# Scoring and summing units of 16 neighbour slots or more in two parts, in both graph-attention layers

## The chip, the cores and the metric

The program runs on one core of a Trainium2 chip. The metric is the device time of one execution in microseconds. Engines are named as in the profile: PE (TensorE, matmuls; PEld its weight loads), DVE (VectorE), ACT (ScalarE), POOL (GpSimd, which here issues the gathers), SP (SyncE, which issues plain DMAs).

## The reference

Two graph-attention layers over 2048 nodes, 8 batches of 256 features, with one adjacency matrix that is sparse (a few to some 36 neighbours a node). Cut to what matters:

```python
def _L0_gnn_ref(inp, adj, W1, W2, W3):
    e = jnp.einsum('bnd,bmd->bnm', inp @ W1, inp @ W2)
    e = jax.nn.leaky_relu(e, 0.2)
    e = jnp.where(adj[None, :, :] > 0, e, NEG_INF)
    attention = jax.nn.softmax(e, axis=-1)
    return jax.nn.relu(jnp.einsum('bnm,bmd->bnd', attention, inp @ W3))

def _L1_gnn_ref(h, adj, W, a):
    q = (h @ W).reshape(B, N, H, D)
    e = e_src[:, :, None, :] + e_dst[:, None, :, :]
    e = jnp.where(e >= 0, e, 0.2 * e)
    e = jnp.where(mask, e, NEG_INF)
    attn = jax.nn.softmax(e, axis=2)
    h_prime = jnp.einsum('bijh,bjhd->bihd', attn, q)
    return jax.nn.elu(h_prime.reshape(B, N, H * D))

x = _layernorm(x + _L0_gnn_ref(x, adj, W1, W2, W3))
x = _layernorm(x + _L1_gnn_ref(x, adj, W, a))
```

## The kernel before

**Units and slots.** The nodes are sorted by their number of neighbours and cut into 16 tiles of 128 nodes. `SLOTS` says how many neighbours the fullest node of each tile may have: 36, 24, 22, 21, 20, 19, 19, 18, 17, 17, 16, 15, 15, 14, 13, 12. A *slot* of a tile is one neighbour of each of its 128 nodes; nodes with fewer neighbours have masked slots, for which `neg` (one value per node and slot) holds a huge negative number and otherwise 0. The batches are taken in two halves of four. A *unit* (`Unit`, L438) is one tile of one half in one layer: 64 units, 2 x 2 x 298 slots in all. Layer 0 takes the tiles from the smallest to the largest, first for one half of the batches and then for the other; layer 1 takes a mixed order, with the 36-slot tile in the middle.

**Gathers and the ring.** A unit's neighbour rows come from DRAM by indirect DMAs that POOL issues, one per slot (128 rows of 4 KB), two slots to a chunk (`chunk_job`, L466; `gather`, L196). A chunk lies in one of 16 ring buffers (`RING`), and is given back once its slots are summed (`credits`). So at most 32 slots are in flight, scored and waiting, or being summed. `pump` (L477) issues gathers as long as there are credits.

**Scoring.** In layer 0 (`logits0`, L552) DVE takes, per slot and batch, the product of the gathered row with the node's own transformed row `u.g` and sums it into one score (L568: a custom operation and a read of its accumulator). When a part's slots are all scored, a chain of small operations makes the softmax: leaky ReLU (L581), the mask added (L582), maximum (L586), subtraction (L587), Exp on ACT (L588), sum (L591), reciprocal and division (L593, L594). In layer 1 (`logits1`, L765) the score is an addition of precomputed terms (L780), 16 values per slot, and the same chain follows at L788 to L810; the probabilities are also copied to PSUM (`pw`, L800).

**Summing.** In layer 0 (`sums0`, L654) ACT writes, per slot, four diagonal matrices from the probabilities (L665, four buffers of one slot each), and PE multiplies the gathered rows with them into PSUM accumulators, 16 matmuls a slot (L645). In layer 1 (`sums1`, L818) the gathered rows are weighted in place, four chunks of five by DVE (L846) and each fifth by ACT (L842), and PE adds them up, 8 matmuls a slot. The accumulators are two PSUM banks a part, from a pool of four.

**Parts.** A unit is split into two parts where it has more than 24 slots: the 36-slot tile alone, 18 + 18. Each part then has its own maximum, unnormalised probabilities and accumulators, and `shares` (L600) computes both parts' factors at the end of the unit, has PE move them to the order of the accumulators' rows (L620), and both accumulators are scaled and added (L683 to L691; L866 to L879). An unsplit unit's accumulators are copied out by ACT in layer 0 (L680) and read directly in layer 1 (L884, L892).

**What follows a unit.** `after0` (L695) transposes the sums, projects them with W3, adds the residual (L705), normalises, computes the layer-1 rows and scatters them (L204). `after1` (L863) does ELU, residual and layer norm and scatters the output. `before0` (L530) prepares the own rows of a unit.

**Order.** `tick` (L961) is called after each summed slot; it issues gathers, advances scoring by up to two steps while fewer than `limit` slots are scored ahead of the sums, and advances the work before and after units. A chunk is scored no earlier than 3 (layer 0) or 5 (layer 1) ticks after its gather. POOL's order is that of the program text; on the other engines a list scheduler fills gaps from this order when the program is built. The call at L998 gives the limit: rest of the unit + the next unit + 5.

Of the kernel before, what the change touches and what calls it, by code (L numbers as in the profile page):

```python
# [38 lines left out]
RING = 16  # L39
LEAD = 5  # L40
# [89 lines left out]
def fast_path(  # L130
# [307 lines left out]
    class Unit:  # L438
        def __init__(self, layer, h, t):
# [3 lines left out]

            n = self.K if self.K <= RING * CHUNK * 3 // 4 else -(-self.K // 2)
            self.parts = [(k, min(n, self.K - k)) for k in range(0, self.K, n)]
# [106 lines left out]
    def logits0(u):  # L552
# [3 lines left out]
        for i, (k0, K) in enumerate(u.parts):  # L556
            n, o = f"{u.name}_{i}", offs[u.t] + k0
            e = ep.tile([P, HB, K], F32, tag="e", name=f"e_{n}")
            for k in range(K):
# [6 lines left out]
                for b in range(HB):  # L566
# [6 lines left out]
                        scalar=0.0,  # L573
                        op0=ALU.mult,
                        op1=ALU.add,
                        accum_out=e[:, b, k : k + 1],
                    )
                yield 1
            p = e
            wide = [P, HB, K]  # L580
            nc.vector.scalar_tensor_tensor(p, e, ALPHA, e, ALU.mult, ALU.max)  # L581
            nc.vector.tensor_tensor(  # L582
                p, p, neg[:, o : o + K].unsqueeze(1).to_broadcast(wide), ALU.add
            )
            m = sp.tile([P, HG], F32, tag="m1", name=f"m_{n}")[:, :HB]
            nc.vector.tensor_reduce(m, p, AX.X, ALU.max)  # L586
            nc.vector.tensor_tensor(p, p, m.unsqueeze(2).to_broadcast(wide), ALU.subtract)  # L587
            nc.scalar.activation(p, p, AF.Exp)  # L588
            yield 0
            sm = sp.tile([P, HG], F32, tag="s1", name=f"s_{n}")[:, :HB]  # L590
            nc.vector.tensor_reduce(sm, p, AX.X, ALU.add)  # L591
            if len(u.parts) == 1:
                nc.vector.reciprocal(sm, sm)  # L593
                nc.vector.tensor_tensor(p, p, sm.unsqueeze(2).to_broadcast(wide), ALU.mult)  # L594
# [5 lines left out]
    def shares(u, G):  # L600


        f = sp.tile([P, 2, HG], F32, tag="f", name=f"f_{u.name}", bufs=1)[:, :, :G]
        top = sp.tile([P, HG], F32, tag="top", name=f"top_{u.name}", bufs=1)[:, :G]
        nc.vector.tensor_tensor(top, u.m[0], u.m[1], ALU.max)
        for i in range(2):
            nc.vector.tensor_tensor(f[:, i, :], u.m[i], top, ALU.subtract)
        nc.scalar.activation(f, f, AF.Exp)
        for i in range(2):
            nc.vector.tensor_tensor(u.s[i], u.s[i], f[:, i, :], ALU.mult)  # L610
        nc.vector.tensor_tensor(top, u.s[0], u.s[1], ALU.add)
        nc.vector.reciprocal(top, top)
        nc.vector.tensor_tensor(f, f, top.unsqueeze(1).to_broadcast([P, 2, G]), ALU.mult)
        fs = sp.tile([P, 2, 2, HG // 2], F32, tag="fs", name=f"fs_{u.name}", bufs=1)
        fs = fs[:, :, :, : G // 2]
        for r in range(2):
            rr = slice(64 * r, 64 * r + 64)
            pf = ps_tile(f"ps_f_{u.name}_{r}")[:, :G].rearrange("p (i g) -> p i g", i=2)
            for c in range(2):
# [3 lines left out]
                    rhs=f[rr, :, ts(c, G // 2)],  # L623
# [4 lines left out]
            nc.vector.tensor_copy(fs[:, :, r, :], pf)  # L628
# [25 lines left out]
    def sums0(u):  # L654
        accs = []
        for i, (k0, K) in enumerate(u.parts):
# [3 lines left out]
            for k in range(K):  # L660
# [10 lines left out]
                if s == n - 1:  # L671
                    credits[0] += 1
                yield 1
            accs.append(acc)

        def evict():
            u.hs = hsp.tile([P, HC], F32, tag="hs", name=f"hs_{u.name}")
            if len(accs) == 1:
                for r in range(2):
                    nc.scalar.copy(u.hs[:, ts(r, HW)], accs[0][r])  # L680
                return
            fs = shares(u, HB)
            for r in range(2):  # L683
                for j in range(2):
                    v = u.hs[:, ts(2 * r + j, C)]
                    nc.scalar.activation(
                        v, accs[0][r][:, ts(j, C)], AF.Copy, scale=fs[:, 0, r, j : j + 1]
                    )
                    nc.vector.scalar_tensor_tensor(
# [614 lines left out]
```

## Time and profile before

| | us |
|---|---|
| median of 14 runs (2641.13 to 2659.82) | 2648.78 |
| the profiled execution | 2650.9 |
| its span, first to last instruction | 2649.1 |
| layer 0 sums, first half of the batches | 170 to 885 |
| layer 0 sums, second half | 885 to 1548 |
| layer 1 sums | 1548 to 2626 |

| engine | busy us | share of the span |
|---|---|---|
| PE | 2090.0 | 79% |
| DVE | 2013.1 | 76% |
| ACT | 1445.0 | 55% |
| POOL | 1520.0 | 57% |

| group | count | busy us | mean ns of one |
|---|---|---|---|
| L568 DVE product and sum, layer 0 | 2384 | 858.5 | 419 |
| L645 PE sums, layer 0 | 9536 | 749.6 | 409 |
| L645 PE sums, layer 1 | 4768 | 847.1 | 672 |
| L846 DVE weighting, layer 1 | 260 | 573.9 | 2228 |
| L665 ACT diagonals, layer 0 | 2384 | 623.4 | 337 |
| L196 POOL gathers, layer 0 / layer 1 | 596 / 596 | 626.3 / 603.9 | 1051 / 1013 |

The stages are read off the sums' matmuls (L645): the first of layer 0 starts at 169.7 us, the first of the second half at 892.1, the first of layer 1 at 1552.3, the last ends at 2625.5. In a row, instructions of one engine overlap a little, so that the mean of one is longer than the time from one start to the next; busy time counts no moment twice. The wait lines give the engine, its line and tile, what ended the wait, the total in us, how often, and the longest. POOL's busy time holds only the issuing of the DMAs, not their transfers.

### The profile page before, as it was taken

What the parts mean: (1) busy time and instruction counts of PE and PEld (TensorE: products, weight loads), DVE (VectorE), ACT (ScalarE), POOL (GpSimd) and SP (SyncE); (2) the same over time, 40 slices, a digit from 0 to 9 for tenths busy, and PEclk for the clock granted to TensorE, in tenths of its full rate; (3) what the DMA queues carried; (4) which work ended last, traced back from release to release, by engine and by line L of the source; (5) the groups of instructions that cost most, each with busy time, mean ns of one, the idle gap of its engine ahead of it and who ended that gap; (6) DMA issues with size and microseconds to landing.
All of it is one profiled execution on the core that took longest, in us unless ns stands there. A gap on an engine that the chain in (4) does not pass through costs nothing.

```text
span 2649.1 us, 52177 instructions
## 1 busy us (share of the span) xinstructions
PE 2090.0 (79%) x16675; PEld 1105.6 (42%) x16675; DVE 2013.1 (76%) x7073; ACT 1445.0 (55%) x4849; POOL 1520.0 (57%) x1486
## 2 busy tenths in 40 slices
PE   0148889888889888889988888877877778887885
PEld 0135555555555555555555533322323223332223
DVE  7779687777878676677878667778877787887886
ACT  6135565655666566766666765442455545542544
POOL 3454455545556444555555647676676666665664
PEclk9578899889999899999999988888889898887888
DMA  9777788878786677888988678877898899868883
GB/s 378 277 266 250 270 287 279 268 273 277 261 294 221 215 241 261 280 296 271 303 293 266 233 251 309 311 289 261 291 322 310 293 327 319 306 239 279 325 306 101
DMA packets 249419, 734.92 MB, mean 277 GB/s; under 512 B 63200, under 2 KB 72544, under 8 KB 246704
## 3 DMA queue, kind: packets, MB, share of 16 engines
q0 software_dynamic: 192512, 645.89, 70.8%
q1 hardware_dynamic: 55360, 84.44, 9.4%
q8 instruction: 135, 2.21, 0.3%
q14 instruction: 148, 1.21, 0.1%
q10 hardware_dynamic: 1264, 1.18, 0.1%
HBM read 708.35 MB, written 76.09 MB: 296 GB/s over the span
## 4 chain that ended last, share of the span: by engine, by line
issue 29%; PE 23%; DVE 16%; DMA 13%; POOL 11%; ACT 3%; another core or an unknown queue 1%; POOLq 1%; DVEq 0%; SPq 0%; ACTq 0%
PE acc L645 19%; POOL s L196 8%; DMA s<-xg,idx 7%; DVE j L568 6%; DMA s<-qg,idx 5%; DVE s L846 4%; ACT dg L665 1%; POOL qg L204 1%; PE ps_p_h L427 1%; DMA nb<-edges,order 1%; POOL out_dram L204 1%; PE ps_q L729 1%; DVE st L384 1%; PE ps_t_x L417 1%
## 5 line engine op out<-in xcount | busy, mean ns | idle before, releaser
L568 DVE CUSTOM_DVE_ANT_0 j<-s,g 128x256 bf16<-128x256 f32 x2384 | 858.5, 419 | 253.3 <-DMA s<-xg,idx 208.9
L645 PE MATMUL acc<-s,ident 64*64 64x512 f32 x4768 | 847.1, 672 | 213.1 <-issue 181.2
L196 POOL DMA_INDIRECT s<-xg,idx x596 | 626.3, 1051 | 582.7 <-PE acc L645 311.9
L645 PE MATMUL acc<-s,dg 64*64 64x256 f32 x9536 | 749.6, 409 | 127.3 <-ACT dg L665 51.4
L196 POOL DMA_INDIRECT s<-qg,idx x596 | 603.9, 1013 | 340.6 <-issue 148.9
L665 ACT ACTIVATE dg<-twice,e 128x64 f32<-128x64 f32 x2384 | 623.4, 337 | 162.2 <-PE acc L645 89.8
L645 PEld LDWEIGHTS acc<-s,ident 64*64 64x64 f32 x4768 | 322.1, 149 | 730.0 <-issue 662.9
L846 DVE TENSOR_TENSOR s<-s,p 128x2048 f32<-128x2048 f32 (+1 forms) x260 | 573.9, 2228 | 0.0
L645 PEld LDWEIGHTS acc<-s,dg 64*64 64x64 f32 x9536 | 396.9, 140 | 420.0 <-issue 194.0
L842 ACT ACTIVATE s<-s,e 128x64 f32<-128x64 f32 x1408 | 346.9, 335 | 73.5 <-issue 29.8
L780 DVE TENSOR_TENSOR e<-s,own 128x32 f32<-128x32 f32 (+1 forms) x306 | 56.8, 187 | 206.7 <-DMA s<-qg,idx 174.1
L568 DVE DVE_READ_ACCUMULATOR2_ANT e<- 128x1 f32 x2384 | 190.7, 80 | 5.8 <-issue 5.7
L395 ACT ACTIVATE z<-st,roots 128x4 f32<-128x4 f32 x64 | 19.0, 298 | 300.2 <-DVE st L384 208.8
L204 POOL DMA_INDIRECT out_dram<-o,oidx x128 | 131.7, 1029 | 64.9 <-issue 31.4
L427 PE MATMUL ps_p_g<-A,xT 128*128 128x256 f32 x512 | 133.2, 405 | 27.4 <-ACT xT L419 24.5
L729 PE MATMUL ps_q<-wqs,x1T 128*128 128x264 f32 x512 | 138.1, 405 | 8.2 <-ACT x1T L419 2.3
L427 PE MATMUL ps_p_h<-w_sb,hT 128*128 128x256 f32 x512 | 129.4, 396 | 0.5 <-ACT hT L419 0.3
L427 PEld LDWEIGHTS ps_p_g<-A,xT 128*128 128x128 f32 x512 | 97.8, 199 | 58.6 <-ACT xT L419 27.6
L729 PEld LDWEIGHTS ps_q<-wqs,x1T 128*128 128x128 f32 x512 | 96.9, 197 | 39.9 <-issue 11.3
L407 ACT ACTIVATE o<-xr,nmr,rstd 128x256 f32<-128x256 f32 x128 | 66.5, 589 | 81.7 <-DVE nmr L403 37.8
L427 PEld LDWEIGHTS ps_p_h<-w_sb,hT 128*128 128x128 f32 x512 | 93.5, 193 | 37.0 <-issue 15.5
L796 ACT ACTIVATE e<-e 128x288 f32<-128x288 f32 (+11 forms) x34 | 14.8, 435 | 171.1 <-DVE m L794 80.4
(138 smaller groups left out, 1483.1 us busy)
## 6 DMA issues: line engine op xcount, KB each, us to landing
adj<-in_adj_dram SPq DMA_DIRECT2D x16, 1024.0 KB
xr<-xo SPq DMA_DIRECT2D x128, 128.0 KB
x1s<-y SPq DMA_DIRECT2D x32, 512.0 KB
xr<-x1s SPq DMA_DIRECT2D x32, 512.0 KB
s<-xg,idx POOLq DMA_INDIRECT x596
s<-qg,idx POOLq DMA_INDIRECT x596
edges<-adj SPq DMA_DIRECT2D x16, 512.0 KB
xg<-in_x_dram SPq DMA_DIRECT2D x4, 2048.0 KB
```

The costliest lines, as they stand in the source:

```text
L196: nc.gpsimd.indirect_dma_start(out=dst, out_offset=None, in_=table, in_offset=AT(ap=index, axis=0), bounds_check=table.shape[0] - 1, oob_i ...
L204: ins = nc.gpsimd.indirect_dma_start(out=table, out_offset=AT(ap=index, axis=0), in_=src, in_offset=None)
L384: nc.vector.bn_stats(st[:, i, :], y[:, 2 * i : 2 * i + 2, :].rearrange("p b c -> p c b"))
L407: nc.scalar.activation(dst[:, b, :], y[:, b, :], AF.Identity, bias=nmr[:, b : b + 1], scale=rstd[:, b : b + 1],)
L427: nc.tensor.matmul(pp[:, ts(j, C)], lhsT=srcT[:, ts((2 * i + j) * KC + k, P)], rhs=weight[:, k, :], start=(k == 0), stop=(k == KC - 1),)
L568: nc.vector.tensor_tensor_reduce(out=jt, in0=rows[:, s, ts(b, C)], in1=u.g[:, ts(b, C)], scale=1.0, scalar=0.0, op0=ALU.mult, op1=ALU.add, ...
L645: nc.tensor.matmul(out, lhsT=lhsT, rhs=rhs, start=(k == 0 and j == 0), stop=(k == K - 1 and (j == 1 or diag is None)), tile_position=(64 * ...
L665: nc.scalar.activation(diag[:, b, :], twice, AF.Copy, scale=u.p[i][:, b, k : k + 1])
L729: nc.tensor.matmul(pq[:, : C + 2 * H], lhsT=x1T[:, ts(i * KC + k, P)], rhs=w.sqs[:, k, j * H : j * H + CD + H], start=(k == 0), stop=(k == ...
L780: nc.vector.tensor_tensor(e[:, c * CHUNK : c * CHUNK + ns, :].rearrange("p s (b g) -> p s b g", b=HB), rows[:, :ns, :].rearrange("p s (b w ...
L842: nc.scalar.activation(v[:, a, g, :], v[:, a, g, :], AF.Copy, scale=pv[:, a, g : g + 1])
L846: nc.vector.tensor_tensor(v, v, pv.unsqueeze(3).to_broadcast([P, n * HB, H, D]), ALU.mult)
```

## The change

A unit of 16 slots or more is now split into two parts (11 of 16 tiles, in both layers), the first with an even number of slots, so that the chunks stay the same. The parts of 36 are 18 + 18 as before; 24 becomes 12 + 12, 22 12 + 10, 21 10 + 11, 20 10 + 10, 19 10 + 9, 18 10 + 8, 17 8 + 9, 16 8 + 8.

The second part's softmax runs over its own scores and the first part's maximum, which is put into an extra column of the score tile; its sum takes in the first part's sum, scaled. So the second part's probabilities come out normalised over both, and the extra column holds the factor by which the first part's accumulators must be scaled. `spread_shares` has PE move these factors to the accumulators' row order, and ACT copies them out. After the fourth slot of the second part has been summed, ACT writes the first part's scaled accumulators into `u.hs`, and at the end DVE adds the second part's accumulators (two additions of 512 columns). In layer 1 the first part's probabilities are copied to PSUM by ACT rather than DVE, and the chunks that ACT weights are counted through both parts.

In layer 0 the mask is no longer added after scoring: it is the start value of each product's sum (L568), for all units. The look-ahead of scoring goes by parts: the rest of the part + the next part + 5.

```diff
+SPLIT = 16
@@ Unit
-            n = self.K if self.K <= RING * CHUNK * 3 // 4 else -(-self.K // 2)
-            self.parts = [(k, min(n, self.K - k)) for k in range(0, self.K, n)]
+            n = self.K
+            if n >= SPLIT:
+                n = CHUNK * ((n + 2) // (2 * CHUNK))
+            self.parts = [(0, n), (n, self.K - n)][: 1 if n == self.K else 2]
@@ logits0
-            e = ep.tile([P, HB, K], F32, tag="e", name=f"e_{n}")
+            last = i == len(u.parts) - 1
+            e = ep.tile([P, HB, 1 + K + 1], F32, tag="e", name=f"e_{n}")
...
-                        scalar=0.0,
+                        scalar=neg[:, o + k : o + k + 1],
...
-            nc.vector.scalar_tensor_tensor(p, e, ALPHA, e, ALU.mult, ALU.max)
+            p = e[:, :, 1 : 1 + K]
+            nc.vector.scalar_tensor_tensor(p, p, ALPHA, p, ALU.mult, ALU.max)
+            v = p
+            if i:
+                v = e[:, :, : 1 + K]
+                nc.vector.tensor_copy(e[:, :, 0], u.m[0])
+            m = sp.tile([P, HG], F32, tag="m1", name=f"m_{n}")[:, :HB]
+            nc.vector.tensor_reduce(m, v, AX.X, ALU.max)
             nc.vector.tensor_tensor(
-                p, p, neg[:, o : o + K].unsqueeze(1).to_broadcast(wide), ALU.add
+                v, v, m.unsqueeze(2).to_broadcast([P, HB, v.shape[2]]), ALU.subtract
             )
...
+            nc.scalar.activation(v, v, AF.Exp)
             yield 0
             sm = sp.tile([P, HG], F32, tag="s1", name=f"s_{n}")[:, :HB]
-            nc.vector.tensor_reduce(sm, p, AX.X, ALU.add)
-            if len(u.parts) == 1:
+            v = p
+            if i:
+                v = e[:, :, 1:]
+                nc.vector.tensor_tensor(e[:, :, 1 + K], e[:, :, 0], u.s[0], ALU.mult)
+            nc.vector.tensor_reduce(sm, v, AX.X, ALU.add)
+            if last:
                 nc.vector.reciprocal(sm, sm)
-                nc.vector.tensor_tensor(p, p, sm.unsqueeze(2).to_broadcast(wide), ALU.mult)
+                v = p if i == 0 else e[:, :, : 1 + K]
+                nc.vector.tensor_tensor(
+                    v, v, sm.unsqueeze(2).to_broadcast([P, HB, v.shape[2]]), ALU.mult
+                )
+                if i:
+                    u.fs = spread_shares(u, e[:, :, 0], HB)
@@ spread_shares, in the place of shares
+    def spread_shares(u, share, G):
+        fs = sp.tile([P, 2, HG // 2], F32, tag="f0", name=f"f0_{u.name}", bufs=2)[:, :, : G // 2]
+        for r in range(2):
+            rr = slice(64 * r, 64 * r + 64)
+            pf = ps_tile(f"ps_f0_{u.name}_{r}")[:, : G // 2]
+            for c in range(2):
+                nc.tensor.matmul(
+                    pf[64 * c : 64 * c + 64],
+                    lhsT=ident[rr, rr],
+                    rhs=share[rr, ts(c, G // 2)],
+                    start=True,
+                    stop=True,
+                    tile_position=(64 * r, 64 * c),
+                )
+            nc.scalar.copy(fs[:, r, :], pf)
         return fs
@@ sums0
+                if i == 1 and k == 3:
+                    u.hs = hsp.tile([P, HC], F32, tag="hs", name=f"hs_{u.name}")
+                    for r in range(2):
+                        for j in range(2):
+                            nc.scalar.activation(
+                                u.hs[:, ts(2 * r + j, C)], accs[0][r][:, ts(j, C)], AF.Copy,
+                                scale=u.fs[:, r, j : j + 1],
+                            )
...
         def evict():
+            if split:
+                for r in range(2):
+                    v = u.hs[:, ts(r, HW)]
+                    nc.vector.tensor_tensor(v, v, accs[1][r], ALU.add)
+                return
@@ logits1
-                nc.vector.tensor_copy(pw, p)
+                nc.scalar.copy(pw, p)
...
+    def scalar_chunks(u, i):
+        k0, K = u.parts[i]
+        return [c for c in range(-(-K // CHUNK)) if (k0 // CHUNK + c) % SHARE == SHARE - 1]
@@ sums1
+                    if i == 1 and c == 1 and s == 1:
+                        u.hs = hsp.tile([P, HC], F32, tag="hs", name=f"hs_{u.name}")
+                        for r in range(2):
+                            for g in range(HG // 2):
+                                nc.scalar.activation(
+                                    u.hs[:, ts(r * HG // 2 + g, D)],
+                                    u.accs[0][r][:, ts(g, D)],
+                                    AF.Copy,
+                                    scale=u.fs[:, r, g : g + 1],
+                                )
@@ after1
-            fs = shares(u, HG)
...
+            v = [u.hs[:, ts(r, HW)] for r in range(2)]
             for r in range(2):
...
-                nc.vector.tensor_tensor(v[r], v[r], v2[:, ts(r, HW)], ALU.add)
+                nc.vector.tensor_tensor(v[r], v[r], u.accs[1][r], ALU.add)
@@ the loop over units
+        ends_of = [u.K - k0 - K for k0, K in u.parts]
+        follow = [K for _, K in u.parts[1:]] + [units[min(j + 1, len(units) - 1)].parts[0][1]]
...
-            tick(left + units[min(j + 1, len(units) - 1)].K + LEAD)
+            i = next(i for i, end in enumerate(ends_of) if left > end or end == 0)
+            tick(left - ends_of[i] + follow[i] + LEAD)
```

## The prediction

> **What bounds the kernel now.** I read the engines' busy time by stage first, since the two layers have different limits: layer 0's first half of the batches (170 to 885 us), its second half (885 to 1548), and layer 1 (1548 to 2626). Of the two scoring rows, the instructions of L568 alone, each product counts twice (the product and the read of its accumulator).
>
> ```profile
> core 0: us, PE busy (x) PEld busy (x) DVE busy (x) ACT busy (x) POOL busy (x), PEclk, DMA share, GB/s
> 170.00:885.00 715.00, 618.27 (x5887) 385.38 (x5880) 574.48 (x3142) 432.41 (x1512) 378.22 (x362) 0.93 0.80 266
> 885.00:1548.00 663.00, 585.11 (x5874) 369.21 (x5873) 479.57 (x2475) 440.89 (x1548) 359.91 (x345) 0.95 0.80 267
> 1548.00:2626.00 1078.00, 861.26 (x4833) 333.14 (x4832) 837.64 (x1130) 504.79 (x1702) 700.76 (x691) 0.85 0.82 290
> ...
> 170.00:885.00 715.00, 448.18 (x2485) 0.93 0.80 266
> 885.00:1548.00 663.00, 394.82 (x2188) 0.95 0.80 267
> ```
>
> In layer 0 PE is the fullest engine (618/715 = 86.5%, 585/663 = 88.3%), with DVE behind it at 80.3% and 72.3%. Then I asked who waits for whom: twice in layer 0, first half and second, and once in layer 1.
>
> ```profile
> DVE j L568 <- DMA s<-xg,idx: 96.1, 63, 4.8
> ...
> POOL s L196 <- PE acc L645: 130.6, 71, 7.6
> ...
> POOL s L196 <- PE acc L645: 194.3, 102, 11.8
> ...
> DVE j L568 <- DMA s<-xg,idx: 111.5, 72, 6.7
> ...
> POOL s L196 <- issue: 145.2, 447, 2.3
> POOL s L196 <- remote: 109.4, 65, 2.7
> POOL s L196 <- PE acc L645: 50.0, 19, 9.7
> ```
>
> In layer 0 the gathers wait for PE to give ring buffers back, and DVE, which scores a chunk as soon as it lands, waits for those late gathers. The ring is full because PE is slow, so DVE's waits are mostly spare time there. Layer 1 is another case: each gather holds POOL 0.99 us and the next follows 0.30 later, so 691 instructions need 701 + 691 x 0.30 = 908 us, and with 109 of "remote" 1017 of the 1078 us are POOL's own supply. Only the 50 us of waiting for PE could go. The largest of them lie behind the two 36-slot units, already in two parts, whose sums hold PSUM until the rescaling on DVE is done:
>
> ```profile
> 1854.23 2.79 PE L645 MATMUL acc<-s,ident 64*64 64x512 f32 x9 [11.00 <-issue]
> ...
> 2433.97 2.79 PE L645 MATMUL acc<-s,ident 64*64 64x512 f32 x9 [15.08 <-issue]
> ```
>
> **The scalar of each score.** The mask moves from an addition after scoring into the start value of every product (L568), so a constant becomes one value per partition. No row shows this custom operation so. Two pairs of other DVE operations show the step. One element takes (2277 - 1210)/1024 = 1.042 ns by the two widths of L846.
>
> ```profile
> 61.91 2.34 DVE L289 TENSOR_SCALAR_CACHE_REDUCE junk<-keys,key 128x2048 f32<-128x2048 f32 x1
> 64.18 0.08 DVE L289 DVE_READ_ACCUMULATOR junk<-keys,key 128x1 f32 x1
> ...
> 905.55 0.46 DVE L356 TENSOR_SCALAR_CACHE_REDUCE listless<-neg 128x298 f32<-128x298 f32 x1
> 905.93 0.08 DVE L356 DVE_READ_ACCUMULATOR listless<-neg 128x1 f32 x1
> ...
> 891.90 1.65 DVE L689 SCALAR_TENSOR_TENSOR hs<-acc,fs,hs 128x256 f32<-128x256 f32 x4
> ...
> 257.82 0.68 DVE L705 SCALAR_TENSOR_TENSOR y<-ps_p_h,xr 128x512 f32<-128x512 f32 x1
> 258.43 0.41 DVE L568 CUSTOM_DVE_ANT_0 j<-s,g 128x256 bf16<-128x256 f32 x1
> ```
>
> The same operation with a per-partition scalar (L289) takes 2.27 - 2.134 = 0.136 us over its elements until the next starts; with a constant (L356) 0.38 - 0.311 = 0.07. The second pair: L689 starts every (1.65 - 0.474)/3 = 0.392 us, 0.125 over its 256 elements; L705, with a constant, 0.61 - 0.534 = 0.076. So a pointer costs 0.05 to 0.066 us; I take 0.06. The bounds are 0 (the custom operation may fetch a constant the same way) and 0.066. L568 now repeats every 0.35 us, so a slot of four rises from 1.39 to about 1.63. Products: 2485/2 = 1242 and 2188/2 = 1094, hence 75 us and 66 us of DVE. The removed addition (34 of about 0.23 alone, 0.15 in a row) gives back some 2 us in each half.
>
> **Small DVE operations.** Ten tiles a half are newly split. In layer 0 the softmax goes from 7 operations of 68 elements (17 slots; 0.17 to 0.24 us alone, about 0.08 less from start to start) to 12 of half the width: 12 x 0.115 - 7 x 0.15 = 0.33 us. The eviction becomes two DVE additions of 512 from PSUM, 0.60 each from start to start like L873. That is 1.5 us a unit, 15 us a half. In layer 1, 15 operations of 136 for 8 of 272 give about 0.5 us, the additions 1.2: 20 x 1.7 = 34 us. The two 36-slot units save six L873/L879 (3.6 us) and gain about half of that back, and move one 2.2 us chunk each to ACT: -8. DVE's new load: 574 + 75 + 15 - 2 = 662 of 715 (93%); 480 + 66 + 15 - 2 = 559 of 663 (84%); 838 + 26 = 864 of 1078 (80%).
>
> [...]
>
> **ACT.** Layer 0: four scaled copies (L686, 0.39 from start to start) for two plain ones of 0.5, two small copies of the shares, one more Exp: about 1.1 us x 22, hidden by ACT's 282 us idle in the first half. Layer 1: 16 scaled copies at L842's pace of 0.24 us, two share copies, one more Exp, one copy of p: about 5 us x 22 = 110 us, under ACT's 573 us idle (505 of 1078 busy). Without that cover it would cost those 110.
>
> **The share matmuls, a new wait on PE.** `spread_shares` puts four tiny matmuls (about 0.19 each, overlapping, 6 us in all for layer 0) into PE's queue right after the softmax of the second part, some two slots into the unit's own sums. Behind them stand the sums of the first part, and behind those the ring and the gathers. The nearest row is ACT's wait for the same softmax:
>
> ```profile
> ACT e L588 <- DVE e L587: 100.8, 23, 21.7
> ```
>
> That is 4.4 us a time. ACT may be four diagonals (four slots, over 4 us) ahead of PE, so PE's own wait lies between 0 and 4.4 us; nearest to 0, and I take 0.3 x 22 = 7 us in layer 0; the bound is 97. In layer 1 PE waits for DVE's weighting anyway: 0. SP's and POOL's queues lose and gain nothing: the chunks are the same in number, for every first part is even.
>
> [...]
>
> **The order of scoring.** Before, the look-ahead is the unit's rest + the next unit + 5 slots (17 + 17 + 5 = 39, over the ring's 32), so scoring is put three steps behind its gather. After, it is the part's rest + the next part + 5 (8 + 9 + 5 = 22), so some ten slots lie between. DVE's 96 + 111 us of waiting for landings should all but vanish; what that frees is needed by the added work.
>
> **The sum.** First half: if the fullest engine stays as full as now, 662/0.865 = 765 us (+50); if the vanished waits let DVE fill 93%, 714 (0). The best of any 100 us before was 84%, but with those waits in it; I take the middle, +25. Second half: PE with the share matmuls 588/0.883 = 666 (+3; ends -20 and +20). Share wait +7. Layer 1: the early scaling frees PSUM, so the 11.0 and 15.1 us behind the 36-slot units can go, but POOL's supply holds the rest: half, -13 (ends -50 and +15). Total +22. The profiled execution is 2650.9 us (span 2649.1 and 1.8 around it), so 2673; it is 2 above the median of 14, hence 2671.
>
> **Rivals.** (a) The looser order wins: layer 0's fullness gains more than DVE's added work takes. For it: DVE's waits for landings are 207 us there, and PE's waits for diagonals 51. Against it: PE idles only 97 + 78. If a quarter of that goes (-44) with all 26 us behind the 36-slot units, 2649 - 70 = about 2580. (b) The pointer is free in the custom operation: DVE's first half holds 587 of 715, the +25 falls away, 2646. For it, L568 already carries two scalars; against it, both pairs. (c) The share matmuls decide: from the point where DVE is more than four diagonals late, PE stops for up to 4.4 us in each of 22 units of layer 0: 2671 + 90 = 2760. For it, DVE at 93%; against it, PE waited only 51 us for the diagonals in 32 units.
>
> **Chances.** Forecast 0.50 (2655 to 2725), (a) 0.20, (b) 0.17, (c) 0.13. About 0.2% (5 us) is what a measurement of this kernel can tell from no change. Faster by more: all of (a), over half of (b), a little of the forecast: 0.32. Same: 0.08, from (b) and the forecast's edge. Slower: 0.60. The range, 2605 to 2750, leaves out half of (a), half of (c) and little else; the forecast's own is 2655 to 2725.
>
> **What would show it.** L568's start-to-start time 0.40 to 0.41 (0.35 would be (b)); DVE's waits for s<-xg under 40 us; DVE over 88% in the first half; waits of PE on the share matmul's line under 20 us (near 90 would be (c)); POOL still issuing without pause in layer 1, its span between 1050 and 1080; PE no longer idle over 10 us behind the 36-slot units. The prediction fails if layer 0 ends earlier than 1540 with L568 lengthened: then fullness, not load, was the limit.

## The result, and the profile after

The changed kernel takes 2747.86 us (median of 10 runs, 2739.15 to 2753.72) against 2648.56 for the kernel before beside it: ratio 1.0375, 95% interval 1.0357 to 1.0393, slower by 99 us. The forecast was +22 and slower. The sign is right, and the time lies just inside the range (2605 to 2750) but above the forecast's own 2655 to 2725. The forecast size is less than a quarter of what came.

First the busy time by stage (span, then us and instructions of PE, PEld, DVE, ACT and POOL, the granted clock, DMA share and GB/s), and under the dots the scoring line alone. The stages are layer 0's two halves and layer 1, cut at their first matmuls.

```profile
169.00:924.00 755.00, 621.26 (x5990) 392.16 (x5989) 662.49 (x3222) 444.45 (x1576) 377.33 (x364) 0.91 0.76 253
924.00:1647.00 723.00, 619.86 (x5941) 385.84 (x5937) 558.42 (x2526) 449.42 (x1599) 357.25 (x345) 0.90 0.75 244
1647.00:2723.00 1076.00, 869.26 (x4994) 327.93 (x4986) 853.15 (x1292) 600.89 (x2198) 702.11 (x691) 0.85 0.83 290
...
169.00:924.00 755.00, 517.53 (x2486) 0.91 0.76 253
924.00:1647.00 723.00, 455.95 (x2184) 0.90 0.75 244
```

Cut in the same way, the kernel before has 722, 660 and 1073 us. So the loss is layer 0's: +33 in the first half, +63 in the second, +3 in layer 1. DVE's load is what the prediction had (forecast 662, 559, 864; found 662, 558, 853). Yet no engine is full: PE has fallen from 86% and 88% of the two halves to 82% and 86%, and DVE stands at 88% and 77%. Something makes the engines wait for each other. The waits of PE and DVE (in all, times, longest, us; the second half's under the dots) include one of PE that the kernel before hardly had:

```profile
PE ps_t_h L419 <- DVE hs L692: 49.5, 8, 9.3
DVE j L573 <- DMA s<-xg,idx: 33.8, 23, 11.4
DVE j L573 <- ACT dg L669: 21.1, 8, 4.1
...
PE ps_t_h L419 <- DVE hs L692: 44.5, 10, 7.2
DVE j L573 <- ACT dg L669: 40.5, 16, 12.8
DVE j L573 <- DMA s<-xg,idx: 32.3, 21, 6.8
```

L692 is the eviction's addition on DVE. The timeline shows why PE's transposes wait for it (start, duration, engine, line, instruction, and the idle time with its releaser):

```profile
1325.68 0.47 DVE L573 CUSTOM_DVE_ANT_0 j<-s,g,neg 128x256 bf16<-128x256 f32 x1
...
1326.90 1.27 DVE L692 TENSOR_TENSOR hs<-hs,acc 128x512 f32<-128x512 f32 x2
1327.73 1.09 PE L419 MATMUL ps_t_h<-ident,hs 128*128 128x128 f32 x4 [3.10 <-DVE hs L692]
...
1328.74 1.98 PE L648 MATMUL acc<-s,dg 64*64 64x256 f32 x14
1328.85 0.59 ACT L421 COPY hT<-ps_t_h 128x512 f32<-128x512 f32 x1 [3.35 <-PE ps_t_h L419]
```

DVE scores without a pause up to 1326.90, and only then comes the addition, 1.27 us for both halves. It stood in DVE's queue behind products of later units. PE idles 3.10 us for it, and ACT stands 3.35 us ahead of its next copy, most of it at the same time. Before, ACT did this eviction, and PE waited for it 5 us in all of layer 0:

```profile
PE ps_t_h L417 <- ACT hs L680: 4.7, 4, 2.1
```

### The profile page after: what moved, and what is told of

It reads as the page before. It is cut to its first block, busy times and chain, and to the rows that moved or that the text cites. A ratio compares the mean times of both kernels' runs of the same rounds, so it can differ in the third digit from the quotient of the medians.

```text
span 2746.5 us, 53804 instructions
## 1 busy us (share of the span) xinstructions
PE 2134.9 (78%) x16995; PEld 1123.4 (41%) x16995; DVE 2195.6 (80%) x7349; ACT 1559.7 (57%) x5451; POOL 1517.1 (55%) x1486
## 3 DMA queue, kind: packets, MB, share of 16 engines
q14 instruction: 155, 1.27, 0.2%
## 4 chain that ended last, share of the span: by engine, by line
DVE 30%; PE 23%; issue 22%; DMA 9%; ACT 7%; POOL 6%; another core or an unknown queue 1%; POOLq 0%; DVEq 0%; ACTq 0%
PE acc L648 17%; DVE j L573 16%; DMA s<-qg,idx 5%; DVE s L872 4%; POOL s L198 4%; DMA s<-xg,idx 4%; ACT s L868 3%; ACT dg L669 2%; PE ps_p_h L429 2%; PE ps_p_g L429 1%; DVE st L386 1%; DVE e L573 1%; PE ps_t_h L419 1%; PE ps_t_x L419 1%; DVE some L510 1%
## 5 line engine op out<-in xcount | busy, mean ns | idle before, releaser
L573 DVE CUSTOM_DVE_ANT_0 j<-s,g,neg 128x256 bf16<-128x256 f32 x2384 | 992.8, 477 | 157.1 <-DMA s<-xg,idx 67.5
L198 POOL DMA_INDIRECT s<-xg,idx x596 | 619.7, 1040 | 698.9 <-PE acc L648 407.7
L648 PE MATMUL acc<-s,dg 64*64 64x256 f32 x9536 | 772.1, 414 | 124.4 <-issue 84.2
L648 PEld LDWEIGHTS acc<-s,ident 64*64 64x64 f32 x4768 | 311.4, 148 | 662.9 <-issue 601.7
L648 PEld LDWEIGHTS acc<-s,dg 64*64 64x64 f32 x9536 | 406.6, 142 | 421.6 <-issue 254.1
L868 ACT ACTIVATE s<-s,e 128x64 f32<-128x64 f32 x1472 | 366.1, 349 | 46.2 <-issue 17.3
L573 DVE DVE_READ_ACCUMULATOR2_ANT e<- 128x1 f32 x2384 | 184.9, 78 | 2.8 <-issue 2.6
L419 PE MATMUL ps_t_h<-ident,hs 128*128 128x128 f32 x256 | 55.4, 355 | 102.2 <-DVE hs L692 94.0
L808 ACT ACTIVATE e<-e 128x160 f32<-128x160 f32 (+9 forms) x54 | 19.0, 352 | 149.1 <-DVE e L805 66.2
```

The source lines that it names most:

```text
L198: nc.gpsimd.indirect_dma_start(out=dst, out_offset=None, in_=table, in_offset=AT(ap=index, axis=0), bounds_check=table.shape[0] - 1, oob_i ...
L419: nc.tensor.transpose(pt[:, ts(j, P)], src[:, ts(4 * i + j, P)], ident)
L573: nc.vector.tensor_tensor_reduce(out=jt, in0=rows[:, s, ts(b, C)], in1=u.g[:, ts(b, C)], scale=1.0, scalar=neg[:, o + k : o + k + 1], op0= ...
L648: nc.tensor.matmul(out, lhsT=lhsT, rhs=rhs, start=(k == 0 and j == 0), stop=(k == K - 1 and (j == 1 or diag is None)), tile_position=(64 * ...
L868: nc.scalar.activation(v[:, a, g, :], v[:, a, g, :], AF.Copy, scale=pv[:, a, g : g + 1])
```

## Experiments

The chips that ran these kernels run the kernel before in 2483 to 2487 us, mostly because layer 1 takes 973 us there rather than 1073. The change costs more on them, so each ratio is against the kernel before on its own chip, and 1% is 25 us. As no profile of the kernel before was taken there, e12, the kernel before with a shorter look-ahead (ratio 1.0007; stages 686, 650 and 973 us) stands in for it below.

| run | what it is | ratio | 95% interval |
|---|---|---|---|
| e5 | the change itself | 1.0495 | 1.0459 to 1.0531 |
| e1 | change, constant start value | 1.0391 | 1.0361 to 1.0421 |
| e2 | before, pointer start value | 1.0093 | 1.0063 to 1.0123 |
| e3 | change, later transposes | 1.0340 | 1.0306 to 1.0374 |
| e4 | change, more score tiles | 1.0584 | 1.0542 to 1.0625 |
| e6 | change, these three together | 1.0340 | 1.0303 to 1.0378 |
| e7 | e6 with the old look-ahead | 1.0662 | 1.0625 to 1.0699 |
| e8 | layer 1's split alone | 1.0019 | 1.0002 to 1.0036 |
| e9 | e1 and e3 together | 1.0227 | 1.0188 to 1.0267 |
| e10 | e9, Exp of layer 0 later | 1.0177 | 1.0133 to 1.0221 |
| e11 | before, Exp of layer 0 later | 0.9982 | 0.9961 to 1.0003 |
| e12 | before, shorter look-ahead | 1.0007 | 0.9989 to 1.0024 |
| e13 | before, ACT copies added | 0.9996 | 0.9976 to 1.0017 |
| e14 | before, ACT made to stand | 1.0196 | 1.0170 to 1.0222 |
| e15 | change in 36-slot units only | 0.9947 | 0.9927 to 0.9967 |
| e16 | e15, Exp of layer 0 later | 0.9900 | 0.9873 to 0.9926 |
| e17 | e16 again | 0.9926 | 0.9905 to 0.9947 |
| e18 | e9, two slots of lead | 1.0221 | 1.0200 to 1.0242 |

### e5: the change on these chips

> The changed kernel as it is, beside the others of this call, so that each has it and the kernel before on one chip. All theories: 1.03 to 1.06 of before. If the eviction's wait (theory E) is the larger part, e3's 1.034 lies at least 0.012 under it; if the pointer (theory P) is, e1's 1.039 does.

Ratio 1.0495: +125 us by the medians, of which layer 0 takes 1456 us against 1336. This is the base for what follows.

### e1 and e2: the pointer as start value

e1, in the changed kernel:

```diff
-                        scalar=neg[:, o + k : o + k + 1],
+                        scalar=0.0,
...
+            nc.vector.tensor_tensor(
+                p, p, neg[:, o : o + K].unsqueeze(1).to_broadcast([P, HB, K]), ALU.add
+            )
```

> The changed kernel with the start value of every product back to the constant 0 and the mask added to the scores again (54 additions). Theory P (the pointer's 0.06 us in each of 2384 products is DVE load, and in layer 0 DVE is now the bound): the product goes back from 477 to 419 ns, DVE loses 138 us, and 55 to 80 of the 99 us go: 2670 to 2693. Theory E (PE waits for the eviction's additions that stand behind scores in DVE's queue; 94 us in the changed kernel's trace): those waits stay over 70 us and the time stays over 2720. Theory T (three score tiles are too few for the parts): over 2720 too, with DVE's 62 us of waiting for the diagonals unchanged.

e2 makes the opposite edit in the kernel before (pointer in, addition out).

> The kernel before with the pointer alone: the mask as start value of every product, its addition taken out, nothing split further. Theory P: 138 us more of DVE load, 50 to 75 us more time: 2700 to 2725. Theory E: DVE's waits for landing gathers (207 us in layer 0) take it up, under 20 us more: below 2670.

Undone, the pointer gives back 1.0495 - 1.0391 = 1.0%, 26 us; alone it costs 0.9%, 23 us. Within their intervals the two agree. The product's duration rises as forecast (419 to 477 ns), and the scoring line's busy time by 517.53 + 455.95 - 448.18 - 394.82 = 130 us over layer 0 (the change against the kernel before), of which about 25 become time. In e1's stages, against e5's, 22 of them are the first half's and 3 the second's; in e2's, against e12's, 14 and 10.

### e3: the eviction's wait

```diff
+        for _ in range(8 if len(u.parts) == 2 else 0):
+            yield
```

This stands at the start of the work that follows a split unit in layer 0 (the transposes of `u.hs` and what hangs on them), and puts it four slots later.

> The changed kernel with the work after a split unit of layer 0 started four slots later, so that other sums stand in PE's queue between the end of a unit and the transposes that need the eviction. Theory E: PE's wait for hs falls from 94 to under 25 us and the time by 50 to 80: 2668 to 2698. Theory P: the wait falls as well, but DVE stays as full, and the time moves into other waits: 2730 to 2750. Theory T: no change but a few us.

PE's wait for L692 falls from 106 us to 8 and the time by 1.5%, 39 us. First e5's line, then e3's:

```profile
PE ps_t_h L419 <- DVE hs L692: 105.6, 20, 9.5
```

```profile
PE ps_t_h L419 <- DVE hs L692: 7.8, 1, 7.8
```

So what cost these 39 us is that PE's next step stood right behind the additions. The additions themselves still run in e3, so what their own 0.68 us each cost is not measured here. Later transposes were not tried in the kernel before; PE waits there only 10 us for its eviction (e12), so little could come of them.

### e4: score tiles

```diff
-            e = ep.tile([P, HB, 1 + K + 1], F32, tag="e", name=f"e_{n}")
+            e = ep.tile([P, HB, 1 + K + 1], F32, tag="e0" if i else "e", name=f"e_{n}")
```

> The changed kernel with three more score tiles in layer 0 (the second parts take theirs from a group of their own). Theory T: DVE's 62 us of waiting for the diagonals' reading of a score tile go, and with them 25 to 50 us: 2698 to 2723. Theories P and E: the waits go, but under 12 us of time: 2736 to 2750.

Wrong in sign: 0.9% slower than the change, intervals apart. These are DVE's waits in layer 0 up to 1500 us, first of the change (e5), then of e4:

```profile
DVE j L573 <- ACT dg L669: 63.1, 26, 7.9
DVE j L573 <- DMA s<-xg,idx: 55.7, 41, 6.0
```

```profile
DVE j L573 <- DMA s<-xg,idx: 185.4, 126, 6.6
DVE j L573 <- ACT g L552: 8.6, 2, 6.1
```

The wait for a free score tile (which the diagonals on ACT give back) is gone, and that for landings has more than tripled. It looks as if DVE now began parts earlier, whose rows are still on their way, and stood there with everything behind it. That this is what costs the time was not tested apart.

### e6 and e7: three undone, and the look-ahead

e6 joins the edits of e1, e3 and e4. e7 adds the old look-ahead:

```diff
-            tick(left - ends_of[i] + follow[i] + LEAD)
+            tick(left + units[min(j + 1, len(units) - 1)].K + LEAD)
```

> The split kept, with the constant start value, the later transposes and the three more score tiles together. Theories P, E and T as one (the layer-0 cost is the sum of these three): within 1.005 of before. Theory S (the split of layer 0 itself: two softmaxes a unit, each with a passage DVE, ACT, DVE, PE, and scoring that starts late by the shorter look-ahead): still over 1.015.

> As the run before, with the look-ahead of the kernel before (rest of the unit + next unit + 5). Theory L (the shorter look-ahead makes DVE score in bursts and late, so that ACT and PE wait for the softmax): at least 0.010 under the run before, ACT's waits for the softmax in layer 0 down by half. If the two softmaxes a unit are it: no change within 0.004.

e6 still stands at 1.034. With split units and these score tiles the old look-ahead costs another 3.2%, 80 us, so the shorter one is no cause of the loss. Of the 80 us, 29 are layer 0's and 52 layer 1's. What the shorter one saves shows at the share matmuls, with which PE moves the factors. PE's waits for DVE there, first in e6, then in e7, with layer 1 under the dots:

```profile
PE ps_f L626 <- DVE e L609: 15.8, 2, 8.2
...
PE ps_f L626 <- DVE e L827: 70.2, 11, 14.5
PE ps_f L626 <- DVE e L792: 63.0, 11, 6.9
```

```profile
PE ps_f L626 <- DVE e L609: 105.0, 18, 8.2
...
PE ps_f L626 <- DVE e L827: 298.8, 21, 17.8
```

That is the wait of the prediction's rival (c), and it grows by far more than the time, so part of it replaces other waits. In layer 0 it comes with the old look-ahead; with the short one it is left in two waits only.

### e8: layer 1's split alone

In layer 0 only the 36-slot units are split (as before) with a constant start value, in layer 1 as in the change:

```diff
-            if n >= SPLIT:
+            if n >= (SPLIT if layer else 25):
```

> Layer 0 split as before (the 36-slot tile alone) with the constant start value; layer 1 split as in the changed kernel. All theories say that the cost is layer 0's: within 0.995 and 1.005 of before, layer 1's stage within 15 us of before's. If layer 1's split costs as well: over 1.008.

1.0019: layer 1's part of the change costs 5 us (0.5 to 9 by the interval), so the rest is layer 0's.

### e9 and e10: do the two costs add, and is ACT's Exp the rest?

e9 joins the edits of e1 and e3. e10 adds, ahead of the Exp in layer 0:

```diff
+            for _ in range(6):
+                yield 0
             nc.scalar.activation(v, v, AF.Exp)
```

> The changed kernel with a constant start value (the mask added after scoring again) and the transposes of split units four slots later in layer 0; the score tiles as in the change. Theory: the pointer's some 25 us and the eviction's wait of some 37 us are separate costs that add, so of the changed kernel's +125 us on these chips some 63 are left: ratio 1.020 to 1.030, layer 0 some 60 us above the 1343 to 1360 of the kernel before. Rival: both act through one late DVE and overlap, then 75 to 90 us are left, ratio 1.031 to 1.037. Since the run with both of these and more score tiles stood at 1.034, the theory also says that the extra tiles cost 20 to 30 us there, the rival that they cost nothing.

> As the run with the constant and the later transposes, and in layer 0 ACT's Exp of each part is emitted some three slots later, behind the diagonals of the slots before it. Theory S (what is left of the loss is ACT standing in its queue at the Exp of a part until DVE has scored it, with the diagonals queued behind it): ACT's waits for DVE at the Exp fall from some 190 to 220 us to under 100, PE's waits for diagonals fall with them, and the time falls by 20 to 40 us. Theory C (the rest is twice as many softmax passages, a shorter supply of rows and PE's lower granted clock): the waits at the Exp move but the time stays within 10 us of the run beside it, or rises, since the weights then come later for the first slot of the part.

e9 came as the theory said: 1.0495 - 0.0104 - 0.0155 = 1.0236 expected from e1 and e3, 1.0227 found, and e6 shows what the extra tiles cost on top (1.1%). e10 is 12 us faster than e9. The intervals of the ratios overlap, but the four runs of each, on one chip, hardly do (2524 to 2536 us against 2535 to 2544), so a small gain is likely. It is less than theory S's 20 to 40 us, and it did not come as that theory says: ACT's waits at the Exp did not fall (192 us in e9, 203 in e10).

Part of what e9 still loses in layer 0, 45 us, shows in who waits. First e8, where these units are whole, then e9 (waits of PE, then of ACT at the Exp):

```profile
PE ps_q L737 <- ACT x1T L421: 5.1, 4, 3.1
...
PE ps_p_h L429 <- ACT hT L421: 1.0, 2, 0.8
...
ACT e L598 <- DVE e L595: 132.3, 28, 10.1
```

```profile
PE ps_q L739 <- ACT x1T L421: 24.3, 17, 2.8
...
PE ps_p_h L429 <- ACT hT L421: 13.9, 6, 4.3
...
ACT e L598 <- DVE e L595: 191.8, 42, 9.6
```

With 54 Exps in layer 0 in place of 34, ACT stands 60 us longer, 42 times in place of 28, and PE's projections wait for ACT's copies of the transposed tiles. The waits of the sums for diagonals did not grow (139.1 us in e8, 110.5 in e9). That points at ACT's queue, and the next pair takes it apart. But waits are not all of it. These are the two halves of layer 0 in e8, then in e9:

```profile
150.00:833.00 683.00, 568.78 (x5913) 366.96 (x5907) 571.30 (x3130) 431.41 (x1522) 384.65 (x368) 0.92 0.83 287
833.00:1485.00 652.00, 561.62 (x5843) 359.02 (x5838) 479.54 (x2477) 437.09 (x1549) 362.33 (x346) 0.94 0.81 271
```

```profile
150.00:847.50 697.50, 582.43 (x5981) 376.41 (x5983) 586.77 (x3226) 439.20 (x1573) 385.57 (x369) 0.92 0.83 280
847.50:1530.50 683.00, 576.58 (x5941) 371.39 (x5933) 498.71 (x2567) 443.48 (x1599) 361.79 (x345) 0.91 0.78 259
```

PE's idle time grows by only 17 of the 45 us. The other 29 are PE being busy longer: 9 of them the added share matmuls, 12 the projections into `ps_q` (0.44 us each in place of 0.40), and the second half runs at a granted clock of 0.91 in place of 0.94.

### e13 and e14: ACT's added work against ACT's standing

Both are the kernel before, whole units. e13 adds four scaled copies in the middle of the sums of the 20 units of 16 to 24 slots:

```diff
+                if len(u.parts) == 1 and K >= 16 and k == K // 2 + 3:
+                    u.hs = hsp.tile([P, HC], F32, tag="hs", name=f"hs_{u.name}")
+                    for b in range(4):
+                        nc.scalar.activation(
+                            u.hs[:, ts(b, C)].rearrange("p (a c) -> p a c", a=2),
+                            ident.unsqueeze(1).to_broadcast([P, 2, P]), AF.Copy,
+                            scale=u.p[i][:, b, k : k + 1],
+                        )
```

> The kernel before, in one part, with four more scaled ACT copies of 256 elements (of a constant, into the tile that the eviction overwrites) in the middle of the sums of the 20 units of 16 to 24 slots in layer 0, where the change puts its rescaling: 20 x some 1.5 us = 30 us of ACT. Theory A (ACT, though 60 to 65% busy in layer 0, makes four diagonals a slot in 0.96 us where PE's slot takes 1.09, so it can't catch up within a unit and its extra work holds PE's transposes and projections): the time rises by 12 to 30 us, ratio 1.005 to 1.012. Rival (ACT's idle time hides it, as the prediction said): under 5 us, 0.998 to 1.002.

e14 adds one copy of 32 elements that can't start before DVE has scored half of the unit:

```diff
+                if len(u.parts) == 1 and K >= 16 and k == K // 2 - 1:
+                    jx = sp.tile([P, HB, 8], BF16, tag="jx", name=f"jx_{n}", bufs=1)
+                    nc.scalar.copy(jx, e[:, :, K // 2 - 8 : K // 2])
```

> The kernel before, in one part, with one more small ACT copy (32 elements) per unit of 16 to 24 slots in layer 0, which reads the scores of the first half: ACT stands in its queue until DVE has scored half of the unit, as the Exp of the first part makes it stand in the change, and nothing else is added but 20 x 0.2 us of ACT. Theory S (the waits themselves cost): the time rises by 8 to 25 us, ratio 1.003 to 1.010. Rival: the waits only shift ACT's idle time, under 5 us, 0.998 to 1.002.

32 us more of ACT's work (448 and 450 us busy against 432 and 434) cost nothing: 0.9996. Twenty copies of 0.22 us cost 2.0%, 49 us, more than both theories said, because each makes ACT stand. ACT's waits in layer 0, and below them ACT's and then PE's timeline around one of the copies:

```profile
ACT jx L580 <- DVE e L568: 114.4, 20, 10.6
```

```profile
612.59 0.57 ACT L548 COPY g<-ps_p_g 128x512 f32<-128x512 f32 x1
623.19 0.22 ACT L580 CAST jx<-e 128x32 bf16<-128x32 f32 x1 [10.03 <-DVE e L568]
623.32 0.37 ACT L740 COPY q<-ps_q 128x264 f32<-128x264 f32 x1
623.59 0.59 ACT L419 COPY hT<-ps_t_h 128x512 f32<-128x512 f32 x1
...
614.82 0.66 PE L417 MATMUL ps_t_h<-ident,hs 128*128 128x128 f32 x4
615.41 1.96 PE L648 MATMUL acc<-s,dg 64*64 64x256 f32 x32
624.23 3.35 PE L427 MATMUL ps_p_h<-w_sb,hT 128*128 128x256 f32 x7 [6.86 <-ACT hT L419]
```

For 10 us ACT does nothing. Behind the little copy stand the copies of q and of hT, whose inputs PE had finished by 615.5, and PE idles 6.86 us until hT is there. Every edit also lets the scheduler order the engines anew; in e11, e12 and e13 this and the edit together move the time by no more than 0.2%. Of the 54 us that e14's layer 0 is longer than e12's, 36 are idle time of PE and 18 are PE busy longer.

### e11, e12: the kernel before with one idea each

e11 takes e10's edit with four steps in place of six, e12 shortens the look-ahead:

```diff
-            tick(left + units[min(j + 1, len(units) - 1)].K + LEAD)
+            i = next(i for i, end in enumerate(ends_of) if left > end or end == 0)
+            tick(follow[i] + LEAD)
```

> The kernel before with the Exp of layer 0 emitted some two slots later. Theory S: ACT's wait at the Exp, 101 us of the first half in the kernel before, is a cost there too, and the time falls by 5 to 20 us: ratio 0.992 to 0.998. Theory C: 0.998 to 1.004.

> The kernel before with the change's shorter look-ahead alone (the rest of the part, the next part and 5 slots). Taking it away from the changed kernel cost some 80 us, so the theory that the shorter look-ahead is itself worth time says that the kernel before gains by it: ratio 0.985 to 0.995. Rival: the look-ahead only has to match the size of the parts; in units of one part it is the same as before except in the two 36-slot units, and the ratio is 0.998 to 1.003.

e12 as it ran goes further than its expectation says. For whole units the change's look-ahead is the old one, so here the rest of the part is dropped too, and the next part and 5 slots are left. The results, 0.9982 with an interval that reaches past 1, and 1.0007, are no gains that can be told: in whole units a shorter look-ahead does nothing, in split ones the old one costs 80 us (e7, with the extra score tiles).

### e15, e16 and e17: the change's form where a split was needed anyway

```diff
-SPLIT = 16
+SPLIT = 25
```

with a constant start value, and in layer 1 the two extra columns of the score tile only in split units, for room. e16 adds e11's edit.

> The changed kernel with only the four 36-slot units in two parts (as before) and a constant start value: the early rescaling of the first part and the softmax over both parts, in the units that were split already. Theory: the change's form is better where a unit must be split anyway; layer 0 stays as in the kernel before, and the 11 to 15 us of PE's idle time behind the 36-slot units of layer 1 shrink: ratio 0.990 to 0.998. Rival: layer 1 is held by the supply of rows and takes it back elsewhere, 0.999 to 1.003.

> As the run with only the 36-slot units in two parts, with the Exp of layer 0 emitted some two slots later. If both small gains are real and add: ratio 0.988 to 0.996, and this is the version that beats both kernels. Rival: the late Exp alone stood at 0.998 with an interval that touches 1, and is nothing: the same as the run beside it within 0.002.

> The same kernel as the run with only the 36-slot units in two parts and the later Exp, again, with more rounds: ratio 0.987 to 0.993 if the gain is real; above 0.996 it was luck.

All three beat both kernels: 0.9947, then 0.9900 and 0.9926 (some 13 and 18 to 25 us). That e16's later Exp adds to it can't be said, since e17's interval overlaps with e15's. Layer 1 by stage in e12 (old form), e15 (new form in the 36-slot units alone) and e8 (new form in all of the change's units):

```profile
1485.00:2458.00 973.00, 621.23 (x4832) 219.46 (x4832) 832.98 (x1125) 496.86 (x1701) 697.66 (x688) 0.81 0.87 320
```

```profile
1484.00:2443.00 959.00, 620.27 (x4830) 217.94 (x4824) 822.43 (x1109) 518.76 (x1798) 704.55 (x691) 0.82 0.89 326
```

```profile
1485.00:2463.00 978.00, 663.49 (x5008) 234.63 (x5004) 851.12 (x1295) 595.64 (x2199) 703.44 (x691) 0.85 0.88 320
```

The new form in the 36-slot units, with its early rescaling, gains 14 us, and splitting the other units takes back 19. Two waits of layer 1 bear on this: POOL's for PE in e12, e15 and e8, and PE's at the share matmuls in e15 and e8 (two lines, for the two operations on DVE that end it).

```profile
POOL s L196 <- PE acc L645: 54.8, 35, 14.2
...
POOL s L198 <- PE acc L651: 34.8, 42, 9.8
...
POOL s L198 <- PE acc L651: 40.9, 38, 10.1
```

```profile
PE ps_f L626 <- DVE e L826: 30.7, 2, 15.7
...
PE ps_f L626 <- DVE e L825: 72.3, 11, 14.5
PE ps_f L626 <- DVE e L790: 61.4, 10, 8.2
```

POOL, which supplies the rows, waits 20 us less for PE in e15. In e8 PE stands 134 us at the share matmuls in place of 31, though its idle time in the whole stage is smaller (314 us against 339), so most of this wait replaces others. How much of the 19 us it is was not separated.

### e18: less lead

```diff
-LEAD = 5
+LEAD = 2
```

> The changed kernel with the constant and the later transposes, and scoring only two slots ahead of what the next part needs instead of five. Theory S (the part of the loss that is left is ACT at the Exps of parts that DVE scores just in time): less lead makes DVE later at the part's boundary, ACT's waits at the Exp grow beyond the 190 us of the run with lead 5, and the time rises by 5 to 25 us over its 1.0227. Rival (DVE scores too early and blocks on gathers that haven't landed, as with more score tiles): its waits for landings fall and the time falls by 5 to 20 us.

1.0221 against e9's 1.0227, with ACT's waits at the Exp at 205 us against 192: no difference in time. Both theories missed; between two and five slots the lead doesn't decide.

## Why the prediction was right or wrong

**The sum.** It was 25 + 3 + 7 - 13 = 22. On the chips of the experiments the +125 are about 25 for the pointer (e1, e2), 38 for the eviction's wait (e3; both together 67, e9), some 45 that splitting layer 0's units costs without these two (e9's 1380 us against 1336), and 5 to 8 in layer 1: some 115 in all, the rest within the intervals. The prediction held only the first.

**The scalar of each score: right in price.** The product grew by 0.058 us where 0.06 was forecast. The +25 of the first half was the middle between 0 and +50 for all of DVE's new load, 75 us of pointer and 15 us of small operations; taking the pointer out gives back 22 there (e1). The second half's +3 was the price of PE's share matmuls and not of DVE's load, so that e1 gives back 3 there is chance; in e2 the halves are 14 and 10. Two of its readings were off: 662/0.93 is 712 and not 714, and DVE's best 100 us before was not 84%, since it is busy 95.14 us from 170 to 270. Rival (b), the free pointer, is out.

**Small DVE operations: the step that failed first.** "The eviction becomes two DVE additions of 512 from PSUM, 0.60 each from start to start like L873." The price is right (1.27 us for two), but only the work was priced. The step moves the eviction from ACT's queue into DVE's, behind scores of later units, and PE's transposes wait for it: 94 us of waits in the profile of the change, some 38 us of time on the other chips (e3). The text did not ask who waits for `u.hs`, although it names what is queued behind the share matmuls.

**ACT: the second step that failed.** Four scaled copies, two copies of the shares and one more Exp were "about 1.1 us x 22, hidden by ACT's 282 us idle in the first half." That is true of the work (e13). But "one more Exp" a unit was priced by its duration, and its price is the wait ahead of it. e14 shows the mechanism by itself at 49 us for 20 waits. That the left 45 us of layer 0 are just this is not shown, and their cause stays open: e9's waits grow by 60 us where e14's grow by 108, only 17 of the 45 are idle time of PE, DVE has some 35 us more of work in e9 than in e8 (40 more additions of the eviction, 27 us, among it), and e10 and e18, which should have moved ACT's waits, did not move them. The row that would have warned stood in the prediction: ACT's wait for the softmax, 100.8 us in 23 waits (one of them, 21.7 us, ahead of the first sums). It was read there as a bound for PE's share matmuls and not for ACT's own queue.

**The share matmuls: right in layer 0, wrong in layer 1.** In the profile of the change PE's waits for DVE on their line are 3.8 and 3.6 us in layer 0, where 7 was forecast. In e9's layer 0 they are 15.5 us, both in the 36-slot units (e8 has 14.0). In layer 1 the wait was put at 0, since PE waits for the weighting anyway. There PE stands at them for 134 us in e8, mostly in place of other waits. Rival (c) gave 2760, near the time that came, by a wait in layer 0 that the change does not have; it appears there with the old look-ahead (e7).

**The order of scoring: right in direction.** DVE's waits for landings fell from 207 to 66 us (forecast under 40). What this freed was not all used: DVE now waits 62 us for score tiles, and ACT and PE wait for DVE. Taking these waits of DVE away by more tiles makes it slower (e4). Rival (a), the gain by a looser order, is out; e7 shows only that the shorter look-ahead keeps the split, with the extra score tiles, from costing 80 us more.

**Layer 1: right in the term, wrong in the sum.** The forecast's -13 is near what e15 finds for the 36-slot units on the other chips (-14). In the profile of the change PE no longer idles behind the first of them, which ends at 1943.7. But it stands 15.89 us inside it, at the share matmuls:

```profile
1904.56 0.40 PE L623 MATMUL ps_f<-e,ident 64*64 64x8 f32 x8 [15.89 <-DVE e L822]
...
1937.17 8.81 PE L648 MATMUL acc<-s,ident 64*64 64x512 f32 x61 [0.80 <-issue]
```

So there the pause moved, and POOL's waits for PE in layer 1 are 48 us where they were 50. The other units' split, put at nothing beyond its DVE load and ACT's covered work, costs 19 on the other chips (e8 against e15); by which wait stays open. On the first chip +3 us came in place of -13.

**Fullness.** The second half's +3 rested on PE staying 88.3% full at its clock. PE's busy time rose from 584 to 620 us for nearly the same matmuls, while the granted clock fell from 0.95 to 0.90 (584 x 0.95/0.90 = 616 is an estimate; that busy time goes by the clock was not shown), and its idle time from 76 to 103 us. So more than half of that half's +63 is PE being busy longer, a term that the prediction did not have.

## What to carry to other kernels

When an edit moves a small step to another engine or adds a small step that waits, price the wait and the queue, not the instruction: ask what stands behind it in its engine's queue, what stands ahead of it, and which engine needs the result next. In e14 ACT waited 10.03 us at a copy of 0.22 us, and the copies of q and hT behind it, whose inputs were finished by 615.5 us, started only after it. ACT's average of 63 to 67% busy in layer 0 (e12) hid 32 us of added work (e13, 0.9996) but not the added waits, 114 us in all (e14, 1.0196), and it pays to try a new form first where the old one already had the cost (e15).

## What the runs showed of the hardware that was not expected

- A start value per partition lengthens the custom product of 256 elements by 58 ns (419 to 477 ns), near the 50 to 66 ns of the prediction's two pairs of stock operations.
- PE's granted clock differed at nearly the same idle time of PE: in the second half of layer 0 it was 0.91 in e9 with 106 us of PE idle and 0.95 in e14 with 98. What set it was not shown, so why the two differ stays open.
- More score tiles made the kernel slower twice (e4 against e5 by 0.9%, e6 against e9 by 1.1%). Both times DVE's waits for landing rows grew, from 56 to 185 us and from 79 to 237; that these waits are the cost is the likely reading.
- The chips differ: the kernel before takes 2649 us on one and 2483 to 2487 on five others, with PE busy 861 us in layer 1 on the first and 621 (e12) for the same matmuls on another. The change costs 3.75% on the first and 4.95% on one of the others.
